# Layer 0's softplus on one core: three VectorE operations a half instead of four, with the rounding and the maximum on ScalarE

## The chip, the core and the metric

The program runs on one core of one Trainium2 chip. A core has a matrix engine (TensorE, PE in the profile), a vector engine (VectorE, DVE), an activation engine (ScalarE, ACT), a general engine (GpSimd, POOL) and queues of transfers (SyncE, SP). Each engine works through its own list of instructions in order, and they wait for each other by semaphores. They work on two on-chip memories, SBUF and PSUM. PSUM is where matrix products land. The metric is the time of one execution on the device in microseconds (us), as the median of several runs.

## The reference, cut to what matters

The model has four layers. Layer 0 is a selective scan, layer 1 a deformable convolution, and layers 2 and 3 are attention with experts. Only layer 0 is touched here. Of it, this is what matters:

```python
x_dbl = jnp.einsum('bkdl,kcd->bkcl', xs, x_proj_w)
dts, Bs, Cs = jnp.split(x_dbl, [R, R + N], axis=2)
delta = jax.nn.softplus(jnp.einsum('bkrl,kdr->bkdl', dts, dt_w) + dt_b[None, :, :, None])
A = -jnp.exp(A_logs)
out_y = _selective_scan(xs, delta, A, Bs, Cs, Ds)
# _selective_scan, one step in time:
dA = jnp.exp(d_t[..., None] * A)
h = h * dA + (d_t * u_t)[..., None] * B_t[:, :, None, :]
y = jnp.einsum('bkdn,bkn->bkd', h, C_t)
```

There are 4 images, 4 directions k, 256 channels (two halves d of 128), 16 states n, and 2304 positions. For each image, direction, channel and state there is one linear recurrence over the positions.

The softplus is computed as max(v, 0) + log(1 + e) with e = exp(-|v|). In single precision 1 + e loses the low bits of a small e, so both versions add a correction: with r = 1 + e as rounded, log(1 + e) is close to log(r) plus the part of e that the rounding dropped, e - (r - 1).

## The kernel before

Layer 0 cuts the work of each image into 12 **pieces**: 4 directions times 3 stretches of `CH` = 768 positions. All four images make 48 pieces. A piece has 16 **steps**, one for each state n, so the main loop (L858) runs over 768 steps g and two more to empty its pipeline. The order of the instructions on PE, ACT, DVE and POOL is the order in which the loop writes them (`tc.manual_schedule`, L835).

One step of the loop does, for the state in hand:

- DVE: the scan of half 0 in two parts. Part 0 (512 positions) reads the PSUM bank `b0`, called b in the profile; part 1 has 256 positions. Then come whatever preparation is due, a product for 2 x 256 positions (`times_b` on VectorE, L527), and the scan of half 1 (768 positions). Scans are L556.
- POOL: a product of 512 positions for half 1 (L523) and a diagonal matrix for the next b (L498).
- PE: 12 transposes of the previous step's states into the bank pair `ps` (L570), 12 transposes back into `yp` (L584), and 8 products that make b of the next step (L530).
- ACT: six scaled copies of `ps` to `hs` (L576), which the transposes back need, and two exponentials dA for the next step (L516).

So PE starts the transposes of a step when DVE has finished the previous one, ACT copies them, PE turns them back and then makes b, and DVE's first scan of the next step needs that b. The ring of the step runs DVE, PE, ACT, PE, DVE.

The **preparation of the next piece** is done meanwhile by a lane. `prepare` (L358) returns a list of items, here 25. The lane `next` (L862) hands them out at `fill()` (L854), which the loop calls three times a step: between two of the back transposes, then twice after `times_b` on PE. I call these places p0, p1 and p2. The list is spread evenly over 39 such places, so over the steps n = 0 to 12 of a piece. A second lane (`image`) hands out the work of the neighbouring image in the same places. In `prepare`:

- `project`, `projected`: the projection to 40 rows, copied to `xd`, and a transfer of 16 rows (`rows`).
- `raw(s, d)` (L397): a product into the single PSUM bank `pu`, 384 positions. `parts(s, d)` (L407) reads it twice: max(v, 0) into `delta` on VectorE (L414) and |v| into `e` on ScalarE (L415). Four such pairs make a piece.
- `exps(d)` (L417): e = exp(-|v|) on ScalarE (L418). `tokens` and `by_token` turn the B and C rows to positions, through the same bank `pu`.
- `rounded(d)` (L420): du = (e + 1) - 1 on VectorE (L423), with `one`, a column of ones spread over the row, as the second tensor. `rest(d)` (L432): du = e - du on VectorE (L434).
- `log()` (L436): e = log(1 + e) on ScalarE for both halves at once (L437).
- `total(d, which)` (L439): adds du, and in another item e, to delta on VectorE (L441).
- `inputs(d)` (L443): du = delta * u on VectorE (L445). `turn`, `turned`: du's half 0 turned by PE and copied by ACT.

By state of the loop (n), the VectorE items fall as follows before the change: L414 one each in n = 2, 3, 4, 5; L423 of half 0 in n = 6; the copy of `by_token`, L434 and L423 in n = 7; L434 in n = 8; L441 in n = 9; L441 and L445 in n = 10; two L441 in n = 11; L445 in n = 12. `collect` (L604) of the piece before lies in n = 3 and 4.

Of the kernel before, what the change touches and what calls it, by code (L numbers as in the profile page):

```python
# [15 lines left out]
F32 = mybir.dt.float32  # L16
I32 = mybir.dt.int32
AF = mybir.ActivationFunctionType
ALU = mybir.AluOpType
# [4 lines left out]
P = 128  # L24
# [15 lines left out]
CH = 768  # L40
# [49 lines left out]
def layer0(env, dr, io, table, offs):  # L90

    with ExitStack() as ctx:
        _layer0(ctx, env, dr, io, table, offs)
# [15 lines left out]
def _layer0(ctx, env, dr, io, table, offs):  # L109
# [7 lines left out]
    nc, tc, ident = env.nc, env.tc, env.ident  # L117
    cp = ctx.enter_context(tc.tile_pool(name="l0c", bufs=1))
# [7 lines left out]
    def load(name, shape):  # L126
        t = cp.tile(shape, F32, name=name)
        nc.sync.dma_start(t, io[name])
        return t
# [23 lines left out]
    opT = load("l0_opT", [P, ND, C])  # L153
    woT = load("l1_woT", [P, TAPS, NOFF])
    bo = load("l1_bo", [NOFF, 1])
    one = cp.tile([P, 1], F32, name="one")
    nc.vector.memset(one, 1.0)

    nc.scalar.activation(A, A, AF.Exp)
    nc.vector.tensor_scalar_mul(A, A, -1.0)  # L160
# [197 lines left out]
    def prepare(x, before_it):  # L358

        k, at = x.k, x.at  # L360
        t = {}

        def u(d, lo, n):
            return (u_wh if k % 2 else u_hw)[:, d, at + lo : at + lo + n]

        def project(s):
            if s == 0:
                t["xd"] = sp.tile([NR + 2 * NS, CH], F32, name="xd", bufs=1)
            t["pp"] = pu.tile([NR + 2 * NS, BLK], F32, name="pu", tag="pu")
            for d in range(ND):  # L370
                nc.tensor.matmul(
                    t["pp"],
                    xpT[:, d, k, :],
                    u(d, s * BLK, BLK),
                    start=d == 0,
                    stop=d == ND - 1,
                )

        def projected(s):
            nc.scalar.copy(t["xd"][:, bass.ts(s, BLK)], t.pop("pp"))  # L380
            if s == CH // BLK - 1:
                x.rows = dr.tile([NS, CH], F32, name="rows", bufs=2)
                nc.sync.dma_start(x.rows, t["xd"][NR : NR + NS, :])

        def tokens():

            n = NR + 2 * NS
            t["bc"] = pu.tile([P, TPC, n], F32, name="pu", tag="pu")
            for m in range(TPC):
                nc.tensor.transpose(t["bc"][:, m, :], t["xd"][:, bass.ts(m, P)], ident[:n, :n])  # L390

        def by_token():
            x.bc = sp.tile([P, TPC, 2 * NS], F32, name="bct")
            nc.vector.tensor_copy(x.bc, t.pop("bc")[:, :, NR:])


        def raw(s, d):  # L397
            t["pp"] = pu.tile([P, BLK], F32, name="pu", tag="pu")
            nc.tensor.matmul(
                t["pp"],  # L400
                dtT[:, k, bass.ts(d, P)],
                t["xd"][:NR, bass.ts(s, BLK)],
                start=True,
                stop=True,
            )

        def parts(s, d):  # L407
            if s == 0 and d == 0:
                x.delta = sp.tile([P, ND, CH], F32, name="delta")
                t["e"] = sp.tile([P, ND, CH], F32, name="e", bufs=1)  # L410
            sub = bass.ts(s, BLK)
            bias = dtb[:, d, k : k + 1]
            pp = t.pop("pp")
            nc.vector.tensor_scalar(x.delta[:, d, sub], pp, bias, 0.0, op0=ALU.add, op1=ALU.max)  # L414
            nc.scalar.activation(t["e"][:, d, sub], pp, AF.Abs, bias=bias)  # L415

        def exps(d):  # L417
            nc.scalar.activation(t["e"][:, d, :], t["e"][:, d, :], AF.Exp, scale=-1.0)  # L418

        def rounded(d):  # L420
            if d == 0:
                x.du = sp.tile([P, ND, CH], F32, name="du")
            nc.vector.scalar_tensor_tensor(  # L423
                x.du[:, d, :],
                t["e"][:, d, :],
                1.0,
                one.to_broadcast([P, CH]),
                op0=ALU.add,
                op1=ALU.subtract,
            )  # L430

        def rest(d):  # L432
            r = x.du[:, d, :]
            nc.vector.tensor_tensor(r, t["e"][:, d, :], r, ALU.subtract)  # L434

        def log():  # L436
            nc.scalar.activation(t["e"], t["e"], AF.Ln, bias=1.0)  # L437

        def total(d, which):  # L439
            dl = x.delta[:, d, :]  # L440
            nc.vector.tensor_add(dl, dl, which[:, d, :])  # L441

        def inputs(d):  # L443

            nc.vector.tensor_mul(x.du[:, d, :], x.delta[:, d, :], u(d, 0, CH))  # L445

        def turn():
            t["pp"] = pu.tile([P, CT // P, P], F32, name="pu", tag="pu")
            for m in range(CT // P):
                nc.tensor.transpose(  # L450
                    t["pp"][:, m, :], x.du[:, 0, x.ct + m * P : x.ct + (m + 1) * P], ident
                )

        def turned():
            x.duT = sp.tile([P, CT // P, P], F32, name="duT")
            nc.scalar.copy(x.duT, t.pop("pp"))  # L456

        def carry():
            x.before = before_it if x.ci else None
            if x.ci < NCH - 1:  # L460
                x.carry = sp.tile([P, ND, NS], F32, name="carry")

        return [
            lambda: project(0),
            lambda: (projected(0), project(1)),
            lambda: projected(1),
            lambda: raw(0, 0),
            lambda: parts(0, 0),
            lambda: raw(0, 1),
            lambda: parts(0, 1),  # L470
            lambda: raw(1, 0),
            lambda: parts(1, 0),
            lambda: raw(1, 1),
            lambda: parts(1, 1),
            lambda: (exps(0), tokens()),
            lambda: exps(1),
            lambda: rounded(0),
            lambda: (by_token(), rest(0)),
            lambda: rounded(1),
            lambda: rest(1),  # L480
            log,
            carry,
            lambda: total(0, x.du),
            lambda: total(0, t["e"]),
            lambda: inputs(0),
            lambda: (turn(), total(1, x.du)),
            lambda: (turned(), total(1, t["e"])),
            lambda: inputs(1),
        ]

# [344 lines left out]
    with tc.manual_schedule(engines=ORDERED):  # L835
# [5 lines left out]
        for s in prepare(pieces[0], None):  # L841
            s()
# [15 lines left out]
        for g in range(len(pieces) * NS + 2):  # L858
            i, n = divmod(g, NS)
            b, p = divmod(i, NPI)  # L860
            if n == 0 and i + 1 < len(pieces):
                lanes["next"] = Lane(prepare(pieces[i + 1], pieces[i]), 3 * (NS - 3))  # L862
# [1529 lines left out]
```

## Time and profile before

| what | value |
|---|---|
| median of the runs shown | 12436.45 us |
| the runs | 12427.92, 12436.45, 12447.01 us |
| the profiled execution | 12545.34 us |
| its span, first to last instruction | 12543.6 us |
| mean clock granted to TensorE | 0.949 |
| busy share of the span, PE / DVE / ACT / POOL | 87% / 68% / 55% / 35% |

The profiled execution took 12545.34 us, 0.9% more than the median, so a sum made in its microseconds is about 0.9% too large for the runs shown.

A row of groups in the profile gives the line, the engine, the operation, the tiles as out<-in, the shapes, the count, and then the busy time in us, the mean of one in ns, the idle time before them, and what ended that idle time. Layer 0's loop runs from 144 us (its first exponential dA) to 5115 us (the last one). A step of the loop takes on average 6.48 us there, from the start of one part-0 scan to the next.

### The profile page before, as it was taken

The page shows a single profiled execution, that of the slowest core. Times are in us where ns is not written, and L with a number is a line of the kernel's source. Part 1 is how long each engine was busy: PE and PEld are TensorE (multiplying, and loading weights), DVE is VectorE, ACT ScalarE, POOL GpSimd, SP SyncE. Part 2 cuts the span into 40 slices and gives each one's busy share as a digit, 9 for nine tenths or more (in the row PEclk, how much of TensorE's full clock was granted, in tenths as well). Part 3 has the DMA queues.
Part 4 walks back from the last instruction along what each step waited for, and adds up shares of the span by engine and source line. Part 5 has one row for each costly group of instructions (what it writes and reads, how often), then busy time and mean ns, then how long its engine had stood idle before and what let it go on. Part 6 is the DMA issues. An engine that isn't in the chain of part 4 may idle for free.

```text
span 12543.6 us, 192625 instructions
## 1 busy us (share of the span) xinstructions
PE 10872.6 (87%) x71008; PEld 8365.3 (67%) x71008; DVE 8487.3 (68%) x15484; ACT 6888.6 (55%) x13190; POOL 4409.7 (35%) x4799
## 2 busy tenths in 40 slices
PE   7788787978887787688879999999999999698897
PEld 6667666766676666588857777777777777333333
DVE  6998989888988899544456656566566565455554
ACT  5777767777777777411135655555556555232332
POOL 2433434333333343366633333333333332100001
PEclk9999999999999999899979999999999999799998
DMA  3221222122212222356500000000000000300003
GB/s 122 68 70 63 80 77 71 63 76 80 70 64 76 79 67 67 111 171 177 170 21 2 4 3 3 4 2 4 2 3 5 1 1 12 115 7 8 8 8 126
DMA packets 329879, 677.51 MB, mean 54 GB/s; under 512 B 41556, under 2 KB 152168, under 8 KB 328048
## 3 DMA queue, kind: packets, MB, share of 16 engines
q1 hardware_dynamic: 276064, 493.50, 12.3%
q0 software_dynamic: 51840, 169.91, 4.8%
q8 instruction: 570, 9.34, 0.3%
q14 instruction: 365, 2.99, 0.1%
q10 hardware_dynamic: 1040, 1.77, 0.0%
HBM read 602.63 MB, written 71.85 MB: 54 GB/s over the span
## 4 chain that ended last, share of the span: by engine, by line
PE 43%; DVE 7%; ACT 3%; issue 1%; DMA 1%; POOL 1%; another core or an unknown queue 0%; SPq 0%; ACTq 0%; DVEq 0%; POOLq 0%
PE psum L1466 4%; PE pt L1003 4%; PE psum L1458 4%; PE pc L1352 3%; PE psum L1402 3%; PE scT L2105 3%; PE sc L2052 3%; PE out L2134 3%; PE psum L1372 2%; PE psum L1212 2%; PE psum L1213 2%; PE psum L1146 2%; PE psum L1290 1%; PE psum L1391 1%; DVE mx L1375 1%
## 5 line engine op out<-in xcount | busy, mean ns | idle before, releaser
L576 ACT ACTIVATE hs<-ps,bct 128x256 f32<-128x256 f32 x4608 | 1853.8, 474 | 1174.9 <-PE ps L570 1122.5
L570 PE MATMUL ps<-ident,h 128*128 128x128 f32 x9216 | 1491.9, 294 | 783.4 <-DVE h L556 612.7
L570 PEld LDWEIGHTS ps<-ident,h 128*128 128x128 f32 x9216 | 1079.7, 148 | 1168.7 <-DVE h L556 720.3
L584 PE MATMUL yp<-ident,hs 128*128 128x128 f32 x9216 | 1399.3, 288 | 28.5 <-ACT ys L599 28.5
L516 ACT ACTIVATE dA<-delta,l_Al 128x768 f32<-128x768 f32 x1536 | 1388.2, 936 | 0.3
L523 POOL TENSOR_TENSOR h<-du,rB 128x512 f32<-128x512 f32 x768 | 1077.5, 1403 | 757.9 <-PE ps L570 683.1
L584 PEld LDWEIGHTS yp<-ident,hs 128*128 128x128 f32 x9216 | 1151.2, 150 | 83.6 <-ACT ys L599 57.6
L556 DVE TENSOR_TENSOR_SCAN h<-dA,h 128x256 f32<-128x256 f32 (+1 forms) x1024 | 1084.4, 1059 | 27.3
L556 DVE TENSOR_TENSOR_SCAN h<-dA,carry,h 128x768 f32<-128x768 f32 x512 | 1027.1, 2006 | 10.5 <-ACT dA L516 10.5
L1206 POOL TENSOR_TENSOR T<-T,bias 128x384 f32<-128x384 f32 x384 | 383.7, 999 | 1563.5 <-DVE fn L1134 1523.2
L498 POOL TENSOR_SCALAR_AFFINE_SELECT dB<-bct 128x512 f32<-128x512 f32 x768 | 746.0, 971 | 358.4 <-PE b L530 240.9
L2113 ACT ACTIVATE pT<-scT 128x768 f32<-128x768 f32 (+2 forms) x504 | 377.6, 749 | 841.0 <-PE scT L2105 838.9
L530 PE MATMUL b<-dB,duT 128*128 128x128 f32 x6144 | 828.3, 279 | 0.8 <-ACT duT L456 0.8
L556 DVE TENSOR_TENSOR_SCAN h<-dA,carry,b 128x512 f32<-128x512 f32 x512 | 645.7, 1261 | 263.1 <-PE b L530 242.7
L1003 PE MATMUL pt<-ident,gw 128*128 128x128 f32 x5184 | 685.1, 294 | 147.2 <-DVE gw L997 117.6
L990 POOL DMA_INDIRECT g<-table,idx x648 | 659.9, 1018 | 390.0 <-DVE gw L997 189.6
L530 PEld LDWEIGHTS b<-dB,duT 128*128 128x128 f32 x6144 | 768.6, 196 | 2.4 <-POOL h L523 1.2
L1003 PEld LDWEIGHTS pt<-ident,gw 128*128 128x128 f32 x5184 | 650.1, 207 | 176.9 <-DVE gw L997 110.6
L997 DVE TENSOR_TENSOR gw<-g,wq 128x512 f32<-128x512 f32 x648 | 428.7, 692 | 496.9 <-PE pt L1003 416.7
L563 POOL COPY carry<-h 128x2 f32<-128x2 f32 x512 | 96.8, 189 | 1782.0 <-DVE h L556 1717.7
L2062 DVE TENSOR_REDUCE mx<-sc 128x2 f32<-128x1024 f32 (+3 forms) x400 | 428.3, 1071 | 345.2 <-PE sc L2052 340.2
L527 DVE TENSOR_TENSOR h<-du,rB 128x512 f32<-128x512 f32 x768 | 638.7, 832 | 1.6 <-DMA rB<-rows 1.4
(394 smaller groups left out, 22833.0 us busy)
## 6 DMA issues: line engine op xcount, KB each, us to landing
rB<-rows SPq DMA_DIRECT2D x768, 384.0 KB
w<-f_w SPq DMA_DIRECT2D x64, 1024.0 KB
table<-zero SPq DMA_DIRECT2D x162, 128.0 KB
table<-tok SPq DMA_DIRECT2D x16, 1152.0 KB
g<-table,idx POOLq DMA_INDIRECT x648
yd<-y SPq DMA_DIRECT2D x4, 2304.0 KB
sums<-raw SPq DMA_DIRECT2D x192, 48.0 KB
xb<-x SPq DMA_DIRECT2D x42, 192.0 KB
```

The costliest lines, as they stand in the source:

```text
L498: nc.gpsimd.affine_select(out=x.dB[n], in_=x.bc[:, m0 : m0 + CT // P, n : n + 1].to_broadcast([P, CT // P, P]), pattern=[[0, CT // P], [1, ...
L516: nc.scalar.activation(dA, x.delta[:, d, :], AF.Exp, scale=A[:, d, x.k, n : n + 1])
L523: nc.gpsimd.tensor_mul(h[:, 1, own], x.du[:, 1, own], x.rB[n][:, own])
L527: nc.vector.tensor_mul(x.h[n][:, :, own], x.du[:, :, own], b)
L530: nc.tensor.matmul(b0[:, bass.ts(m, P)], x.duT[:, m, :], x.dB[n][:, m, :], start=True, stop=True,)
L556: nc.vector.tensor_tensor_scan(h, da, b, initial=first, op0=ALU.mult, op1=ALU.add)
L570: nc.tensor.transpose(tt[:, m, bass.ts(d, P)], x.h[n][:, d, bass.ts(2 * q + m, P)], ident)
L576: nc.scalar.activation(hs, tt[:, m, :], AF.Copy, scale=x.bc[:, 2 * q + m, NS + n : NS + n + 1])
L584: nc.tensor.matmul(yp[:, q, (2 * d + m) * P : (2 * d + m + 1) * P], hs[:, bass.ts(d, P)], ident, is_transpose=True, start=n == 0 and m == ...
L990: nc.gpsimd.indirect_dma_start(out=g, out_offset=None, in_=table, in_offset=bass.IndirectOffsetOnAxis(ap=idx[:, j : j + 1], axis=0),)
L1003: nc.tensor.matmul(pt[:, t - t0, :], gw[:, q, :], ident, start=q == 0, stop=q == 3)
L1458: nc.tensor.matmul(pg, y.w["w1"][:, bass.ts(f, P)], t["uT"], start=True, stop=True)
```

## The change

The maximum goes from VectorE to ScalarE (a Relu with the same bias). The rounding r = 1 + e goes to ScalarE too, and r itself stays in du, not r - 1. VectorE then computes (r - 1) - e in one operation, into e. The logarithm is taken of r, in place, without a bias. At the end `total(d)` subtracts e from the logarithm and adds the result to delta, both in one item. `one` is gone. The list of items is rearranged and has 24 items instead of 25.

```diff
-    one = cp.tile([P, 1], F32, name="one")
-    nc.vector.memset(one, 1.0)
...
             pp = t.pop("pp")
-            nc.vector.tensor_scalar(x.delta[:, d, sub], pp, bias, 0.0, op0=ALU.add, op1=ALU.max)
+            nc.scalar.activation(x.delta[:, d, sub], pp, AF.Relu, bias=bias)
             nc.scalar.activation(t["e"][:, d, sub], pp, AF.Abs, bias=bias)
...
         def rounded(d):
             if d == 0:
                 x.du = sp.tile([P, ND, CH], F32, name="du")
+            nc.scalar.add(x.du[:, d, :], t["e"][:, d, :], 1.0)
+
+        def rest(d):
+            e = t["e"][:, d, :]
             nc.vector.scalar_tensor_tensor(
-                x.du[:, d, :],
-                t["e"][:, d, :],
-                1.0,
-                one.to_broadcast([P, CH]),
-                op0=ALU.add,
-                op1=ALU.subtract,
+                e, x.du[:, d, :], -1.0, e, op0=ALU.add, op1=ALU.subtract
             )
 
-        def rest(d):
-            r = x.du[:, d, :]
-            nc.vector.tensor_tensor(r, t["e"][:, d, :], r, ALU.subtract)
-
         def log():
-            nc.scalar.activation(t["e"], t["e"], AF.Ln, bias=1.0)
-
-        def total(d, which):
-            dl = x.delta[:, d, :]
-            nc.vector.tensor_add(dl, dl, which[:, d, :])
+            nc.scalar.activation(x.du, x.du, AF.Ln)
+
+        def total(d):
+
+            log, dl = x.du[:, d, :], x.delta[:, d, :]
+            nc.vector.tensor_sub(log, log, t["e"][:, d, :])
+            nc.vector.tensor_add(dl, dl, log)
...
             lambda: (exps(0), tokens()),
             lambda: exps(1),
             lambda: rounded(0),
-            lambda: (by_token(), rest(0)),
-            lambda: rounded(1),
+            lambda: (by_token(), rounded(1)),
+            lambda: rest(0),
             lambda: rest(1),
             log,
             carry,
-            lambda: total(0, x.du),
-            lambda: total(0, t["e"]),
+            lambda: total(0),
             lambda: inputs(0),
-            lambda: (turn(), total(1, x.du)),
-            lambda: (turned(), total(1, t["e"])),
+            turn,
+            lambda: (turned(), total(1)),
             lambda: inputs(1),
         ]
```

## The prediction

> **What bounds the kernel now.** I read the slices of the span first, to see which engine is full in layer 0 (the first 16 of 40 slices; digits are tenths of busy time).
>
> ```profile
> PE   7788787978887787688879999999999999698897
> ...
> DVE  6998989888988899544456656566566565455554
> ACT  5777767777777777411135655555556555232332
> ```
>
> VectorE stands at 8 to 9 tenths there, ScalarE at 7. The sums over the loop of layer 0 (start, then busy us per engine) say the same:
>
> ```profile
> 144.00:5115.00 4971.00, 4028.77 (x28336) 3366.38 (x28336) 4419.16 (x4320) 3646.05 (x7080) 1978.81 (x2124) 0.95 0.23 71
> ```
>
> VectorE is busy for 4419 of 4971 us, ScalarE for 3646 (73%). Next, who waits for whom in this stretch (total us, times, longest):
>
> ```profile
> ACT hs L576 <- PE ps L570: 1120.6, 757, 7.8
> ...
> PEld ps L570 <- DVE h L556: 719.1, 434, 7.7
> ...
> DVE h L556 <- PE b L530: 358.8, 215, 6.2
> ...
> DVE h L556 <- ACT dA L516: 38.0, 15, 4.7
> ```
>
> VectorE's main wait is for b. TensorE waits for the scans, ScalarE for the transposes. So the step is a ring with two lengths: VectorE's own list, and the path scan, transposes, hs, transposes back, b. The longer one sets each step. Last, the groups of the softplus, by shape (busy us, mean ns):
>
> ```profile
> L516 ACT ACTIVATE dA<-delta,l_Al 128x768 f32<-128x768 f32 x1536 | 1388.2, 936 | 0.3
> L415 ACT ACTIVATE e<-pu,l_dtb 128x384 f32<-128x384 f32 x188 | 109.2, 581 | 0.0
> ...
> L418 ACT ACTIVATE e<-e 128x768 f32<-128x768 f32 x94 | 79.4, 845 | 0.0
> L437 ACT ACTIVATE e<-e 128x1536 f32<-128x1536 f32 x47 | 69.8, 1484 | 0.0
> ```
>
> and on VectorE:
>
> ```profile
> L414 DVE TENSOR_SCALAR delta<-pu,l_dtb 128x384 f32<-128x384 f32 x188 | 111.1, 591 | 0.6 <-PE pu L399 0.6
> ...
> L423 DVE SCALAR_TENSOR_TENSOR du<-e,one 128x768 f32<-128x768 f32 x94 | 104.1, 1107 | 0.0
> L434 DVE TENSOR_TENSOR du<-e,du 128x768 f32<-128x768 f32 x94 | 102.5, 1090 | 0.0
> ```
>
> **What VectorE loses.** Four maxima of 591 ns and two roundings a piece. A rounding's mean is 1107 ns, its median 951. The timeline shows why:
>
> ```profile
> 2567.96 2.03 DVE L423 SCALAR_TENSOR_TENSOR du<-e,one 128x768 f32<-128x768 f32 x1
> ```
>
> It ran while GpSimd's product L523 ran (2567.30 to 2569.17). The Trainium skill, "SBUF — State Buffer", section "Who interferes with whom", says that a VectorE instruction with two SBUF inputs contends with a GpSimd instruction that reads SBUF. By the mean, all of the 1107 ns would go: 4 x 0.591 + 2 x 1.107 = 4.58 us a piece, 220 us in 48 pieces. By the rule GpSimd's product stays and holds up the next two-input operation instead, as in the step that starts at 2578.83, where L527 took 1.77 us and not its usual 0.68. I take the median: 4 x 0.591 + 2 x 0.951 = 4.27 us, **205 us** in all. The other counts stay: two rests (another opcode; L423 and L434 cost the same), four in `total`, two in `inputs`. The ones' memset (59 ns, once) is nothing.
>
> **What ScalarE gains.** Four Relus: the nearest row is L415, same shape, source and bias, 581 ns. Two additions of 128x768: between L418 (845 ns) and L516 with a column operand (936); I take 845, as the constant is not a column of data. 4 x 0.581 + 2 x 0.845 = 4.01 us a piece, 193 us (201 at the upper end). The logarithm without bias costs the same.
>
> A rule speaks against this: "ScalarE: Activation LUTs", "Rules for kernel authors", sends relu, max and add to VectorE, not ScalarE, for VectorE is up to about 3x faster in bf16. The rows decide here: in fp32 the maximum takes 591 ns on VectorE and |v| of the same tile 581 on ScalarE, the rounding 951 against 845. By the rule, 193 us would be added to save less; by the rows, equal work goes from an engine at 89% to one at 73%, which becomes about 79% ((3646 + 193) of some 4870).
>
> **Where it lies.** The total does not decide, the steps do. From the trace I took, for each of the 767 steps, its length (part-0 scan to the next), VectorE's idle time in it, and when the last b product ended. With 24 items over 39 places, item i comes at place floor(1.625 i): the roundings both land in n = 7 (p0, p1), both rests in n = 8, the logarithm in n = 9, sub, add and L445 in n = 10, sub and add in n = 11. Means by n in us; "late" is the share of steps whose scan starts within 0.15 us of b's end, so that TensorE ended them:
>
> ```
> n   VectorE list      step  idle  late  new step counted
> 2   -1 max            6.02  0.63  0.71  -0.31
> 3   -1 max            6.60  0.20  0.25  -0.40
> 4   -1 max            6.79  0.35  0.25  -0.56
> 5   -1 max            6.26  0.90  0.52  -0.47
> 6   -1 rounding       6.71  0.84  0.42  -0.41
> 7   -rest -rounding   7.18  0.15  0.00  -1.76
> 8   +1 rest           6.24  0.22  0.25  +0.84
> 9   -1 total          6.26  0.26  0.21  -0.73
> 10  +1 add            6.79  0.07  0.15  +0.98
> ```
>
> The new step is the larger of VectorE's list (step less idle, plus or minus the operation) and b's old end plus 0.11 us, step by step; a removed rounding counts at most 951 ns, an added operation 1.05 us. n = 11 keeps two operations. The sum is -2.83 us a piece, **-136 us** in 48: of 205 us a third is lost because b ends the step next.
>
> Against that:
> - **Sub and add are now neighbours and dependent.** A dependent scan starts 0.03 us after its forerunner ends (2566.14 to 2566.17), an independent operation 0.08 us before (2566.92, 2566.84). Two new pairs a piece: 2 x 0.11 x 48 = +11 us.
> - **New waits in n = 4 and n = 5.** raw(1,1) now follows parts(1,0) directly (p2 behind p1), and the transposes of `tokens` follow parts(1,1). Both use the one bank pu, so TensorE stands until ScalarE has done Relu and |v|. Behind it in its queue are the next step's transposes. In a quick step dA ends and parts begin some 4.1 us in, so they end at 5.3 and tokens at about 6.1, with the counted n = 5 at 5.8. ScalarE has exps(0) behind them too. I put 0.3 us for n = 5 to 6 and 0.2 for n = 4: +25 us, bounds 0 and 85 (the sum below with these delays).
> - **ScalarE's other additions are hidden by its wait for the transposes**, 1.2 to 2.6 us idle a step. n = 7 takes 1.69 us more, and shrinks by 1.76, with 2.38 idle: about 1.1 us spill into n = 8, which grows and loses the logarithm. The logarithm (1.48) spills from n = 9 into n = 10, which has 2.48 us idle and grows too. If this cover fails, rival 2 holds.
> - The rests and totals wait for ScalarE a step later than it was asked; nothing. No transfer or GpSimd instruction is moved.
>
> Sum: -136 + 11 + 25 = **-100 us** on the profiled 12545.34; times 12436.45/12545.34, -99: **12,337 us**.
>
> **Rivals.**
> 1. All of VectorE's time counts, because TensorE's path gets shorter with it: b is often late only because the clock was halved after a long VectorE step (granted 0.95 on the mean). -205, so 12,233. For: no VectorE idle in n = 7 and 10. Against: late shares of 0.4 to 0.7 in n = 2, 5, 6. Chance 0.10.
> 2. **Slower: ScalarE becomes the late engine.** Its queue is in order, and the six hs copies (2.48 us in one chain) lie on b's path. Each Relu or rounding ahead of them delays b by its whole length as soon as ScalarE's gap in that step is used up. If I charge b of n = 2 to 6 with 0.58 (1.16 in n = 5), n = 7 and 8 with 1.69, n = 9 and 10 with 1.48 and take the larger as above, the sum is +103 us: 12,538. It decides once ScalarE's idle time of 1.3 to 1.7 us in n = 2 to 6 is gone. For: hs waited for no transpose in a third of the steps n = 6 and 7, so ScalarE was late itself. Against: 1121 us of waiting by hs in the whole. That the Relu brings table loads (1283 ns each at L697) is the other way to get here; L415's |v| and the copies run without one, so a small part of it. Chance 0.18.
> 3. The ring swallows nearly all: delays of one operation only in the step behind give -51 us, with 0.3 and 0.6 us more in n = 5 and 6 -18: 12,385 to 12,419. Chance 0.20.
>
> **Numbers.** The forecast, -55 to -150 us, has 0.52; its own range is 12,287 to 12,382. A measurement of this kernel can tell about 0.2%, 25 us, from no change. Faster: 0.52 + 0.10 + 0.11 of rival 3 = 0.73; same 0.09; slower 0.18. The range leaves out the far end of rival 1 and most of rival 2: 12,245 to 12,445.
>
> **What would show it.** No L414-like row on VectorE; VectorE's busy time in layer 0 down by about 205 us, ScalarE's up by about 193. n = 7 near 5.4 us, n = 10 near 7.8. VectorE's wait for b up from 359 us, ScalarE's wait for ps down. Wrong if the wait of "ps" or "pu" for ScalarE grows by more than 100 us, if new table loads appear, or if n = 2 to 6 get no shorter.

## The result, and the profile after

The changed kernel takes 12345.06 us (median of 4 runs, 12341.56 to 12346.31), against 12433.08 us before (4 runs, 12427.92 to 12447.01). The ratio is 0.9929, with a 95% interval of 0.9917 to 0.9942. So it is 88 us faster; 99 us were forecast (12,337 us).

The two profiled spans differ by more, 12543.6 and 12344.2 us. Taken apart by layer (first to last TensorE instruction of each), layer 0 took 5227.9 and 5144.0 us, 84 us less. Layer 1, which the change does not touch, took 1014.7 and 912.0 us. That part does not go with the kernel: a second profile of the changed kernel had 913.5 us there, and four kernels profiled on a chip where the kernel before took 12,539 us had 1017 to 1029 us. So I compare traces by the **loop of layer 0**, from the first part-0 scan to the last. It took 4968.8 us before and 4885.7 us after, and 4887.9 us in the second profile of the changed kernel, the one repetition: it came back within 3 us. A smaller difference between two traces says nothing.

The slices after the change, in the rows shown before:

```profile
PE   7788788878887787799789999999999998699897
...
DVE  6987878887888889655555665666665665445554
ACT  5877777777777788411145565555555565233332
```

VectorE has lost a tenth in half of the sixteen slices of layer 0, ScalarE has gained one in four. The sums over the loop (start, length, busy us of PE, weight loads, DVE, ACT, POOL):

```profile
144.00:5032.00 4888.00, 3966.59 (x28337) 3309.93 (x28338) 4198.77 (x4038) 3799.24 (x7362) 1959.67 (x2124) 0.96 0.23 73
```

VectorE is busy for 220 us less (4419 to 4199), ScalarE for 153 us more (3646 to 3799). In place of the maximum and the rounding stand, in the groups of ScalarE and VectorE:

```profile
L413 ACT ACTIVATE delta<-pu,l_dtb 128x384 f32<-128x384 f32 x188 | 109.3, 581 | 0.0
L417 ACT ACTIVATE e<-e 128x768 f32<-128x768 f32 x94 | 79.8, 848 | 0.0
L422 ACT ACTIVATE du<-e 128x768 f32<-128x768 f32 x94 | 79.0, 841 | 0.0
```

```profile
L426 DVE SCALAR_TENSOR_TENSOR e<-du,e 128x768 f32<-128x768 f32 x94 | 94.3, 1034 | 0.0
```

The Relu costs 581 ns and the addition 841, as priced; no table load came with them. These rows make 188 us, but busy time counts an overlap once, and each of the 282 operations overlaps its neighbour by 0.1 us or so; that is why ScalarE gained 153 us and not the 193 counted. The waits of the same rows as before:

```profile
ACT hs L571 <- PE ps L565: 903.7, 616, 5.8
...
PEld ps L565 <- DVE h L551: 521.3, 350, 7.1
DVE h L551 <- PE b L525: 469.2, 260, 6.4
...
PEld ps L565 <- ACT hs L571: 396.3, 708, 6.8
...
PE ps L565 <- ACT hs L571: 164.1, 157, 6.5
...
PEld pu L398 <- ACT e L414: 64.9, 106, 1.7
```

VectorE waits more for b (359 to 469 us), TensorE less for VectorE's scans (719 to 521 in the row of loads), ScalarE less for the transposes (1121 to 904). That is the ring turned as forecast. But TensorE waits more for ScalarE. At `ps` the row of loads went from 335.4 to 396.3 us and the row of products from 99.6 to 164.1; the two overlap in time, so TensorE's own wait grew by 61 us. At `pu` the loads waited almost nothing before, and wait 103 us now: the 64.9 shown, and 38.2 at the transposes of `tokens` (L388).

By steps, as in the prediction, from the two traces (mean step in us; idle is VectorE's):

```
n            step before  after   change  counted   idle before  after
2               6.02       5.80   -0.22    -0.31        0.63      1.00
3               6.60       6.12   -0.48    -0.40        0.20      0.42
4               6.79       6.82   +0.02    -0.56        0.35      0.85
5               6.26       6.23   -0.03    -0.47        0.90      1.35
6               6.71       6.41   -0.30    -0.41        0.84      1.64
7               7.18       5.46   -1.72    -1.76        0.15      0.49
8               6.24       6.99   +0.75    +0.84        0.22      0.21
9               6.26       5.81   -0.45    -0.73        0.26      0.67
10              6.79       7.73   +0.93    +0.98        0.07      0.11
11, 12         13.30      13.10   -0.20       0         0.62      0.43
0,1,13,14,15   31.47      31.43   -0.04       0         7.24      7.20
```

The sum is -1.73 us a piece, -83 us in 48 pieces, which is the loop. In n = 7 to 12 the table came out nearly line by line. In n = 4 and 5 nothing was gained: VectorE had 0.59 us less to do and idled 0.5 us longer.

### The profile page after: what moved, and what is told of

The parts are those of the page before. It is cut to its first block, busy times and chain, and to the rows that moved or that the text cites. A ratio compares the mean times of both kernels' runs of the same rounds, so it can differ in the third digit from the quotient of the medians.

```text
span 12344.2 us, 192660 instructions
## 1 busy us (share of the span) xinstructions
PE 10768.3 (87%) x71008; PEld 8255.8 (67%) x71008; DVE 8274.0 (67%) x15195; ACT 7048.2 (57%) x13478; POOL 4441.2 (36%) x4799
## 4 chain that ended last, share of the span: by engine, by line
PE 39%; DVE 7%; ACT 3%; POOL 3%; issue 3%; DMA 3%; SPq 0%; DVEq 0%; ACTq 0%; POOLq 0%
PE psum L1461 4%; PE psum L1453 4%; PE pc L1347 3%; PE psum L1397 3%; PE scT L2100 3%; PE sc L2047 3%; PE out L2129 3%; PE psum L1367 2%; POOL g L985 2%; PE psum L1207 2%; PE psum L1208 2%; DMA g<-table,idx 2%; PE psum L1141 2%; PE psum L1285 1%; PE psum L1386 1%
## 5 line engine op out<-in xcount | busy, mean ns | idle before, releaser
L565 PE MATMUL ps<-ident,h 128*128 128x128 f32 x9216 | 1457.5, 291 | 662.3 <-DVE h L551 433.0
L579 PE MATMUL yp<-ident,hs 128*128 128x128 f32 x9216 | 1359.6, 282 | 28.5 <-ACT ys L594 28.5
L579 PEld LDWEIGHTS yp<-ident,hs 128*128 128x128 f32 x9216 | 1114.7, 146 | 82.4 <-ACT ys L594 58.9
L493 POOL TENSOR_SCALAR_AFFINE_SELECT dB<-bct 128x512 f32<-128x512 f32 x768 | 714.2, 930 | 362.4 <-PE b L525 243.5
L985 POOL DMA_INDIRECT g<-table,idx x648 | 709.1, 1094 | 242.6 <-issue 149.2
L998 PEld LDWEIGHTS pt<-ident,gw 128*128 128x128 f32 x5184 | 610.2, 194 | 149.9 <-DVE gw L992 116.4
L522 DVE TENSOR_TENSOR h<-du,rB 128x512 f32<-128x512 f32 x768 | 613.1, 798 | 0.0
```

Source lines behind the costliest of these rows:

```text
L493: nc.gpsimd.affine_select(out=x.dB[n], in_=x.bc[:, m0 : m0 + CT // P, n : n + 1].to_broadcast([P, CT // P, P]), pattern=[[0, CT // P], [1, ...
L522: nc.vector.tensor_mul(x.h[n][:, :, own], x.du[:, :, own], b)
L565: nc.tensor.transpose(tt[:, m, bass.ts(d, P)], x.h[n][:, d, bass.ts(2 * q + m, P)], ident)
L579: nc.tensor.matmul(yp[:, q, (2 * d + m) * P : (2 * d + m + 1) * P], hs[:, bass.ts(d, P)], ident, is_transpose=True, start=n == 0 and m == ...
L985: nc.gpsimd.indirect_dma_start(out=g, out_offset=None, in_=table, in_offset=bass.IndirectOffsetOnAxis(ap=idx[:, j : j + 1], axis=0),)
L998: nc.tensor.matmul(pt[:, t - t0, :], gw[:, q, :], ident, start=q == 0, stop=q == 3)
```

## The experiments

The first theory was the prediction's: each step is as long as the longer of VectorE's list and the path to b, ScalarE's additions are hidden, and what is lost in n = 4 and 5 is lost to the waits for the one bank `pu`. The rivals: all of VectorE's time counts, or ScalarE has become the late engine. In each table below "2-6" and "7-12" are the steps of a piece summed over these n, in us; "loop" is layer 0's loop in the trace. Before: 32.38, 39.77, loop 4969. Changed: 31.38, 39.09, loop 4886.

### One part alone: e1_max_only and e2_round_only

e1 is the kernel before, with

```diff
-            nc.vector.tensor_scalar(x.delta[:, d, sub], pp, bias, 0.0, op0=ALU.add, op1=ALU.max)
+            nc.scalar.activation(x.delta[:, d, sub], pp, AF.Relu, bias=bias)
```

and e2 is the changed kernel with that line turned back.

> The kernel before, with the maximum alone moved to ScalarE as a Relu; the rounding, the list and its places stay. Theory (each step is the larger of VectorE's list and the path to b): of the 4 x 0.59 us a piece, the step table leaves 1.74 us, less some delay by the later Relu in the queue, so 40 to 80 us under the kernel before, about 12,375. Rival 1 (all of VectorE's time counts): 113 us less, about 12,320. Rival 2 (ScalarE becomes the late engine): 0 or slower, 12,433 and above.

> The changed kernel with the maximum put back on VectorE; the rounding on ScalarE and the new list stay. Theory: the steps n = 6 to 12 keep what they gained (about 1.0 us a piece in the changed kernel's trace), so 35 to 60 us under the kernel before, about 12,388; with the maximum-only run the two gains add up to roughly that of the whole change. Rival 1: 91 us less, 12,342. If the waits for the single bank pu behind ScalarE are what eats the maximum's gain, TensorE's wait for ScalarE at pu is far below the 141 us of the changed kernel here.

| kernel | time, before beside it | ratio, 95% interval | 2-6 | 7-12 | loop |
|---|---|---|---|---|---|
| e1 | 12518.24, 12538.98 | 0.9982, 0.9976 to 0.9989 | 31.92 | 39.82 | 4952 |
| e2 | 12479.39, 12538.98 | 0.9951, 0.9937 to 0.9965 | 31.73 | 39.37 | 4915 |

The rounding and its new list are worth 54 us of the loop, at the upper end of what was expected; TensorE's wait at `pu` is 39 us in the rows of loads, against 103 in the changed kernel. The maximum alone is worth 16 us of the 113 that it took from VectorE, less than any figure of the theory but above rival 2's zero. On top of e2 it brings 29 us. No run has the new list alone.

### Not the bank: e3_old_places

The changed kernel, with the places of the items written out, and three of them moved back (the lines with a minus give the place that the even spread gave):

```diff
-            11: lambda: raw(1, 0),
-            13: lambda: parts(1, 0),
+            10: lambda: raw(1, 0),
+            12: lambda: parts(1, 0),
...
-            16: lambda: parts(1, 1),
+            15: lambda: parts(1, 1),
```

> The changed kernel, with the items raw(1,0), parts(1,0) and parts(1,1) put back in the places which they had before the change, so that no product or transpose into pu directly follows the two ScalarE operations that free the bank. Same instructions. Theory: TensorE's wait for ScalarE at pu falls from about 141 us to under 50, the steps n = 4 and 5 get 0.2 to 0.3 us shorter each, and the time is 15 to 30 us under the changed kernel, about 12,322. Rival: TensorE only waits there instead of for the scans, so the time stays within 8 us of 12,345.

Measured: 12461.19 us beside 12538.98, ratio 0.9942 (0.9929 to 0.9956); 2-6 is 31.53, 7-12 is 39.15, the loop 4894. The wait for the bank went away as expected, in its largest row and in the others:

```profile
PEld pu L398 <- ACT e L414: 37.6, 101, 0.6
...
PE pu L398 <- ACT e L414: 14.6, 85, 0.4
...
PEld pu L388 <- ACT e L414: 8.4, 25, 0.4
```

These three were 64.9, 38.1 and 38.2 us. But n = 4 and 5 stayed at 6.86 and 6.20 us, and the loop is 9 us longer, not shorter. So taking most of the bank's wait away gains nothing in this form, and that step of my reasoning fell. The run does not clear the bank altogether: the moved Relu and |v| now stand ahead of a dA in ScalarE's queue, and what one gains the other may lose.

### ScalarE's queue: e7_double_relu and e10_no_max

In the traces I then looked at when the first of the six hs copies starts after the step's start, and how often it starts with ScalarE not having waited at all: then ScalarE, not the transposes, was late. Before and after, that share in n = 3, 4, 6 was 0.12, 0.19, 0.31 against 0.48, 0.44, 0.54. In n = 5 it was 0.06 both times: there the transposes were late, and not the queue. The mean start in n = 3 to 6 went from 1.79, 1.61, 1.54, 2.14 us to 2.02, 2.01, 1.91, 2.57.

One such step, n = 3 of the same piece, on ScalarE's timeline (start, length). Before, the step starts at 2023.51:

```profile
2025.13 2.49 ACT L576 ACTIVATE hs<-ps,bct 128x256 f32<-128x256 f32 x6
2027.51 0.58 ACT L415 ACTIVATE e<-pu,l_dtb 128x384 f32<-128x384 f32 x1
```

and after, where it starts at 1988.18:

```profile
1987.60 0.59 ACT L414 ACTIVATE e<-pu,l_dtb 128x384 f32<-128x384 f32 x1
1988.06 0.95 ACT L511 ACTIVATE dA<-delta,l_Al 128x768 f32<-128x768 f32 x1
1988.88 0.69 ACT L268 ACTIVATE xn<-pf,l_ln_b,l_ln_g 128x384 f32<-128x384 f32 x1
1989.44 0.96 ACT L511 ACTIVATE dA<-delta,l_Al 128x768 f32<-128x768 f32 x1
1990.27 2.51 ACT L571 ACTIVATE hs<-ps,bct 128x256 f32<-128x256 f32 x6
```

The copies start 1.62 us into the step before, 2.09 after, in both cases straight behind the work ahead of them. |v| of the step before ends only as the step begins, because a Relu went ahead of it, and dA, the neighbouring image's xn and dA queue behind it. VectorE's next step then starts without a wait before, and with one after:

```profile
2029.31 1.19 DVE L556 TENSOR_TENSOR_SCAN h<-dA,b 128x512 f32<-128x512 f32 x1
```

```profile
1992.55 1.06 PE L525 MATMUL b<-dB,duT 128*128 128x128 f32 x8
1993.13 0.59 ACT L414 ACTIVATE e<-pu,l_dtb 128x384 f32<-128x384 f32 x1
1993.71 1.22 DVE L551 TENSOR_TENSOR_SCAN h<-dA,b 128x512 f32<-128x512 f32 x1 [0.40 <-ACT e L414]
```

The profile names |v| as what ended this wait, but |v| ended at 1993.72, after the scan had started. b ended at 1993.61, and the scan followed 0.1 us later as it does behind every b. So this is a wait for b. The same holds for all 45 waits of the scans that the changed kernel's profile puts down to |v|, 34.5 us: they belong to the row of b.

Two runs test this. In e7 the Relu stands twice; in e10 neither engine makes the maximum, so its delta is not the softplus.

```diff
             nc.scalar.activation(x.delta[:, d, sub], pp, AF.Relu, bias=bias)
+            nc.scalar.activation(x.delta[:, d, sub], pp, AF.Relu, bias=bias)
```

```diff
-            nc.scalar.activation(x.delta[:, d, sub], pp, AF.Relu, bias=bias)
...
-            nc.vector.tensor_add(dl, dl, log)
+            nc.vector.tensor_add(dl, log, log)
```

> The changed kernel with each Relu done twice: 111 us more for ScalarE in n = 2 to 5, nothing else. If ScalarE's additions are hidden by its wait for the transposes, as the prediction has it: less than 25 us over the changed kernel. If ScalarE is late in n = 3 to 6 (the copies started with no wait in 0.44 to 0.54 of those steps): 50 to 110 us over it, which undoes most of the gain.

> The changed kernel without the maximum, on either engine: it leaves out max(v, 0), so delta is not the softplus; the last addition reads the logarithm twice, so VectorE's steps n = 6 to 12 stay as they are. It shows what the maximum costs the steps n = 2 to 6 where it is. They sum to 31.4 us a piece in the changed kernel, 32.4 before (a rounding of VectorE among them). If ScalarE being late there is what ate the gain: 0.8 to 1.7 us a piece less, the loop of layer 0 40 to 80 us shorter, near 4830 us, and the first hs copy of n = 3 to 6 back at the start it had before. If another engine (TensorE or GpSimd) ends these steps anyway: the sum stays within 0.3 us, the loop near 4880.

| kernel | time, before beside it | ratio, 95% interval | 2-6 | 7-12 | loop |
|---|---|---|---|---|---|
| e7 | 12434.99, 12438.09 | 0.9998, 0.9990 to 1.0007 | 33.03 | 39.14 | 4969 |
| e10 | 12324.57, 12430.29 | 0.9918, 0.9902 to 0.9935 | 30.86 | 39.24 | 4868 |

The second Relu cost 83 us of the loop out of its 111, and nearly all of it in 2-6 (+1.65 us a piece of 2.32). The first copy moved to 2.45, 2.47, 2.47 and 2.87 us, and VectorE's wait for b, in the waits of e7, grew with it:

```profile
DVE h L552 <- PE b L526: 588.6, 334, 6.7
...
PEld pu L398 <- ACT e L415: 120.4, 111, 2.3
...
PEld pu L388 <- ACT e L415: 56.3, 46, 2.1
```

So an addition to ScalarE in these steps is not hidden; a second Relu is paid at three quarters. By which way is open. It lengthens ScalarE's queue, but it also holds the bank `pu` longer: TensorE's wait there grew from 103 to 177 us in the rows of loads. The share of copies that start without a wait rose in n = 4 alone (0.44 to 0.67; n = 3, 5 and 6 have 0.54, 0.06 and 0.54). In n = 5, which lost 0.68 us, the copies waited for late transposes as before. No run adds to the queue without holding the bank.

e10 says how much the maximum costs where it is: against e10, VectorE's version (e2) costs 46 us of the loop and ScalarE's (the changed kernel) 17 us. The first copies of e10 start at 1.85, 1.84, 1.72 and 2.22 us, two to four fifths of the way back. My expectation of 40 to 80 us for e10 was too high: n = 4 and 5 stay at 6.71 and 6.10 us with the maximum on neither engine. Most of the gain counted for them was not there to be had. So ScalarE's Relus account for the smaller part of what was missing, about a third: in n = 2 to 5, 1.74 us a piece were counted, 0.71 came, and without any maximum 1.03 would have come.

### One or two maxima back: e4_half_relu and e9_last_max_back

The changed kernel with one or two of the four maxima back on VectorE; e4 has `if s:`, e9 `if s and d:` ahead of it.

```diff
+            if s:
+                nc.vector.tensor_scalar(x.delta[:, d, sub], pp, bias, 0.0, op0=ALU.add, op1=ALU.max)
+            else:
+                nc.scalar.activation(x.delta[:, d, sub], pp, AF.Relu, bias=bias)
```

> The changed kernel, with the maximum of the second two blocks (n = 4 and 5) back on VectorE and that of the first two (n = 2 and 3) on ScalarE. Theory: VectorE was idle 0.85 and 1.35 us in n = 4 and 5 of the changed kernel, so its 0.59 us are nearly hidden there, and the bank pu comes free 0.58 us sooner: 0 to 25 us under the changed kernel, about 12,333. Rival 1 (all of VectorE's time counts): 57 us over the changed kernel, 12,402.

> The changed kernel with one maximum of four, that of n = 5, back on VectorE; the other three stay on ScalarE. The double-Relu run showed ScalarE late in n = 3 to 6, and VectorE was idle 1.35 us in n = 5. If that is the cause: n = 5 and 6 together 0.4 to 0.6 us shorter a piece, the loop of layer 0 about 4863 us instead of 4886, ratio to before 0.990. If every operation of VectorE counts: the loop 28 us longer, about 4914.

e4: 12457.42 us beside 12538.98, ratio 0.9933 (0.9920 to 0.9947), 2-6 at 31.13, 7-12 at 39.37, loop 4886. e9: 12331.33 beside 12428.75, ratio 0.9920 (0.9907 to 0.9934), 31.24, 39.35, loop 4889. Neither differs from the changed kernel. e4 fell on the lower edge of its bounds. e9 missed: its gain of 0.4 to 0.6 us in n = 5 and 6 came out as 0.23 (6.41 to 6.13 in n = 6, 6.23 to 6.28 in n = 5) and was given back in n = 4 and 7 to 9. Moving one maximum from an engine to the other changes these steps by little in either direction.

### Two orders of the same work: e6_copies_first and e5_levelled

e6 lets the hs copies pass one of the two exponentials dA:

```diff
-            do(decay, g + 1, 0)
             do(turn, g - 1, 0)
...
             do(turn, g - 1, 2)
+            do(decay, g + 1, 0)
```

> The changed kernel, with the exponential of half 0 (dA for the next step, 0.94 us) behind the six hs copies in ScalarE's queue and not ahead of them. Same instructions. If ScalarE's late start of the hs copies is what eats the maximum's gain in n = 4 to 6, the first copy there comes 0.3 to 0.6 us sooner and the time is 15 to 50 us under the changed kernel. Rival: the wait only moves to VectorE, whose scan then waits for dA (10 to 38 us so far, then over 100), and the time stays or grows.

It is slower: 12565.84 us beside 12438.09, ratio 1.0100 (1.0084 to 1.0115), loop 5106. The first expectation missed. Of the rival, the time grew as it said, but not by the wait that it named: the scan waited 21 us for dA. The copies of n = 3 to 6 start later (2.60, 2.86, 3.07, 3.15 us), though in n = 3, 4 and 6 less often without a wait. ScalarE's wait for the transposes is longer, not shorter, and TensorE's at `pu` is more than twice the 103 us:

```profile
ACT hs L571 <- PE ps L565: 1146.0, 711, 5.5
DVE h L551 <- PE b L525: 727.5, 372, 6.3
...
PEld pu L398 <- ACT e L414: 150.0, 122, 2.6
...
PEld pu L388 <- ACT e L414: 75.5, 47, 2.4
```

It fits that dA ahead of the copies fills time in which ScalarE waits for the transposes anyway, and behind them holds up the parts, the bank and so TensorE. That the bank's part in this cost something is likely, not shown. That letting the copies pass is no remedy is shown; that every order would fail is not.

e5 deals out VectorE's operations one a step, over 45 places, with the logarithm in two halves and the maxima in the places of e3:

```diff
+            23: lambda: rest(0),
+            24: lambda: log(0),
+            26: lambda: rest(1),
+            27: lambda: (log(1), subtract(0)),
...
+            30: lambda: add(0),
+            33: lambda: inputs(0),
...
+            36: lambda: (turned(), subtract(1)),
+            39: lambda: add(1),
+            42: lambda: inputs(1),
```

> The changed kernel once more, as the measure for the others of this chip. Ratio to the kernel before 0.992 to 0.994. Layer 0's loop in its trace 4886 us within 5 us; layer 1, which the change doesn't touch, differs from execution to execution (1015 us in the profiled run of before, 912 in that of the changed kernel) and carries no part of the gain.

> The changed kernel with its VectorE operations dealt out one a step over n = 7 to 14 (sub and add as items of their own, the logarithm in two halves, 45 places instead of 39, the maxima in the places of before); the same elements are computed by the same engines, with one more logarithm instruction a piece. Theory (each step is the larger of two lengths): n = 8, 10 and 11, which are VectorE's, give up 1 to 1.7 us each and n = 9, 13 and 14 take 0.2 to 0.6: 50 to 110 us under the changed kernel, ratio to before about 0.986. Rival 1 (VectorE's total counts): within 15 us of the changed kernel.

The changed kernel again: 12339.23 beside 12438.09, ratio 0.9916 (0.9903 to 0.9930), loop 4888, as expected. e5: 12313.56, ratio 0.9895 (0.9880 to 0.9910), loop 4864. It gained 24 us of the loop, less than half of the least expected. n = 8, 10 and 11 gave up 0.69, 1.75 and 0.61 us as expected, but n = 7, 9, 13 and 14 took 0.89, 0.58, 0.74 and 0.39. I had taken VectorE's mean idle time in n = 13, 0.72 us, for room. It is not spread evenly. In 27 of the 48 steps of n = 13 VectorE idled under 0.15 us, with b ready about 4.2 us into the step. There the added operation made the step 5.87 us long instead of 4.98. The idle time sat in the other 21.

### A version that beats both: e8_both

e5's order, the last maximum on VectorE, and the exponentials of e later, so that ScalarE has less in n = 5 and 6 (the lines with a minus are e5's; most items behind these move back by one to three places as well):

```diff
-            17: lambda: (exps(0), tokens()),
-            18: lambda: (exps(1), rounded(0)),
-            21: lambda: rounded(1),
+            17: tokens,
+            18: lambda: exps(0),
+            21: lambda: (exps(1), rounded(0)),
...
+            24: lambda: rounded(1),
```

> A try to beat both: the levelled kernel with the maximum of n = 5 back on VectorE and the exponentials of e one step later, so that ScalarE has 1.2 us of preparation at most in n = 5 and less in 6. Expected: what levelling gave (24 us of the loop) plus what the run with one maximum back gives (about 23 us), so the loop about 4840 us, ratio to before 0.987 to 0.989. If ScalarE isn't the late engine in n = 3 to 6, no more than the levelled kernel's 4864 us.

12303.43 us beside 12428.75, ratio 0.9896 (0.9881 to 0.9911), loop 4851. The copies of n = 6 start at 2.00 us and that step is down to 6.05 from 6.41. The loop is 35 us shorter than the changed kernel's and 13 us shorter than e5's, where 24 were hoped for. By its time it is 28 us below e9 on the same chip, and e9 was not told apart from the changed kernel. From e5 it is not told apart by its time. As it changes three things at once, it does not show which of them helped.

## Why the prediction was right, point by point

- **What VectorE loses.** Right. Its busy time fell by 220 us, and 205 were counted.
- **What ScalarE gains.** The prices were right, 581 and 841 ns, with no table loads; busy time grew by 153 us and not 193, as the sum of the rows counts overlaps twice. The rows of this kernel decided rightly against the rule of the Trainium skill, "ScalarE: Activation LUTs", "Rules for kernel authors", that keeps relu and add on VectorE: the time fell.
- **The rounding's steps, n = 7 to 12.** Counted -0.67 us a piece, +0.22 for the two dependent pairs; measured -0.68. Of these pairs only one was new. In n = 11 the two L441 of before already depended on each other, through delta: the second started 0.034 us after the first had ended, just as add behind sub does now. n = 11 got 0.06 us shorter. n = 10 has the new pair, and came out at +0.93 where +0.98 was counted without it. The rounding also takes its part of n = 6. e2 shows the rounding with the new list: 54 us.
- **The maximum's steps, n = 2 to 6.** This is the term that was mis-sized: -2.15 counted (n = 6's rounding among it), +0.5 for delays, so -1.6; measured -1.00. Of the 1.74 us counted for the maximum in n = 2 to 5, 0.71 came. Two steps of the prediction made it too large. The smaller is "ScalarE's other additions are hidden by its wait for the transposes": leaving the Relus out (e10) gives 0.32 us a piece in these steps, 17 us of the loop in all, and a second Relu is paid at three quarters (e7).
- **"b's old end plus 0.11 us."** This is the larger one, and e10 shows its size: with the maximum on neither engine, 0.71 of the 1.74 us still did not come, most of it in n = 4 and 5. The end of b after the step's start is not fixed. A likely reason, argued and not shown, is that where several steps in a row get shorter, ScalarE and TensorE start each of them with more of the last one left to do, as the copies' starts show (1.61 us in n = 4 before, 1.84 in e10), and b comes later by that. In n = 7, 8 and 10 the rule held within 0.1 us. In n = 9, a step alone between two longer ones, it missed by 0.28 us, which this reason does not cover.
- **The new waits at pu.** They appeared, as the prediction said they would. Moving the items out of their way gained nothing (e3), while longer holds of the bank go with a longer loop (e7, e6). So what they cost in the changed kernel stays open. The 25 us put down for them fall short of what n = 2 to 6 lost.
- **Rival 1** (-205 us) is out: 88. **Rival 2**, ScalarE late, is true in part of n = 3 to 6 and did not decide the sum, as the rounding brought 54 us and the maximum did not turn into a loss. The sign that I had named for being wrong, TensorE's wait for ScalarE at ps or pu up by more than 100 us, did come, at `pu`: 103 us from nearly nothing. At `ps` it grew by 61 us, and e10, which has no Relu, has most of that too:

```profile
PEld ps L564 <- ACT hs L570: 384.8, 707, 6.9
```

So the sign came although the forecast held, and the wait at `ps` says little of the Relus.

That the sum came so close owes something to luck: n = 2 to 6 fell short by about 31 us, and 11 us charged for dependent pairs were not seen. Why n = 4 and 5 gain so little even in e10 is argued from the copies' starts, not shown by a run that frees TensorE as well.

## What to carry to other kernels

Where one engine is at nine tenths and another at seven, totals do not say what moving work across is worth; look at each step. Here 591 ns less for VectorE gained 0.22 and 0.48 us in n = 2 and 3, and nothing in n = 4 and 5. Mean idle time is not room: it may sit in a part of the steps (n = 13). Doubling a moved operation (e7) and leaving it out (e10) take one run each and show its price from both sides. But ask what else the doubled one holds, here a PSUM bank: the price then has two causes. And where two waits of one engine overlap, their rows are not added.

## What was not expected of the hardware

- **TensorE's clock changed with the steps.** It is halved in stretches of mostly 3.4 us. In n = 8 these took 1.43 us a step before and 0.15 after, when the step ahead of it, n = 7, fell from 7.18 to 5.46 us; in n = 9, now behind the longer n = 8, they grew from 0.54 to 0.91. But n = 11, behind the longer n = 10, stayed at 1.5 us. Over the loop 502 us were at half clock before, 359 after. TensorE was busy for 4.87 of the 7.18 us of n = 7 before, and for 4.37 of 5.46 after. It fits that a long step of VectorE leaves TensorE idle and the next step finds it slow; no run tests it.
- **Other VectorE operations became a little quicker, for a reason that is open.** L527, now L522, took 832 ns on the mean before and 798 after. One would put this down to the removed rounding, which has two inputs and can meet GpSimd's product. But with the maximum alone moved (e1) it took 810 ns, with the rounding alone (e2) 815.
- **One layer's time seems to go with the chip.** Layer 1, whose indirect transfers run on GpSimd's queue, took 904 to 915 us in seven profiles on three chips and 1017 to 1029 in four on another chip, from the same code; the cause is not known. A profile from one chip and a median from another cannot be subtracted.
